# Decay order, seven half-depth products for the shared expert of chunks three and four, and reordered fills at the branch and in the second layer's first chunk

## The chip, the cores and the metric

One Trainium2 chip, of which the kernel uses one core. The metric is the device time of one execution in microseconds (us), the median of three runs. All values are fp32.

## The reference, cut to what matters

There are two layers over 2048 tokens (8 sequences of 256) of 512 features. Each layer normalizes its input and adds two branches to it, an attention and a mixture of experts.

```python
xn = _layernorm(x)
x = x + L0_attn(xn) + L0_ffn(xn)
xn = _layernorm(x)
x = x + L1_attn(xn) + L1_ffn(xn)
```

Layer 0's attention is linear attention with 32 heads of 128 in blocks of 32 tokens, with an exponential decay for each head (`exp(-slope * distance)`). Layer 0's FFN routes each token to two of 16 experts and adds a shared expert:

```python
logits = xt @ router_w + router_b
scores = softmax(logits) + router_bias     # then the best 2 of 4 groups, the best 2 experts in them
h = silu(xt @ w1 + b1) * (xt @ w2 + b2)    # for each expert, times its gate
...
z = silu(xt @ sw1 + sb1) * (xt @ sw2 + sb2) @ sw3 + sb3
```

The shared expert has `sw1` and `sw2` of 512 x 256: together one product of depth 512 and 512 columns for each token. Layer 1 has a softmax attention with one head of 128, and 64 low-rank experts of rank 16, of which each token takes 16:

```python
h = einsum('nd,krd->nkr', xf, A)
out = einsum('nkr,kdr->nd', h * G[:, :, None], B)
```

## The kernel before, in words

Tokens are worked in four chunks of 512 (`CH`), each of four tiles of 128 rows. TensorE (PE) multiplies 128x128 weights with up to 512 columns into PSUM banks, named ps_a (two), ps_b, ps_e, ps_sc (three) and ps_o. VectorE (DVE), ScalarE (ACT) and GpSimd (POOL) do the rest, and nearly all DMAs are issued by SyncE (SP), whose queue is served in the order written.

**The opening** (L144 to L495) is ordered by the tile scheduler: it weighs the instructions by its own costs, and only those under `keep_in_program_order` are held to the order of the code. For each chunk `normalize` (L264) centres and scales the rows, `turn` (L464) transposes them on TensorE (L279) and copies them to `xT` (DVE L284, ACT L282). `shared_up` (L365) computes the shared expert's two products with `project` (L358 to L363): four blocks of 128 features, each four matmuls 128x512 over the depth, 16 matmuls for a chunk; ACT takes silu with the bias (L375), DVE multiplies (L376). Between the blocks stand the router's `scores` (L312). `route` (L321) picks the two experts by a chain of some forty small DVE operations with one exponential on ACT. `share` (L393) and `shared_down` (L379, matmuls L384) make the shared expert's output one chunk later, add it to the rows and store it to `xr`. `decays` (L401) makes the heads' decays, `exp` of `dist` by ACT (L406), and stores them to DRAM in `dec`; `dist` itself is made by POOL (L219 to L235). `token_sums` (L413) makes sums of quarters of xT for the attention's products by sevens: POOL subtracts (L101 is the helper of every such operation), and the results go to DRAM in `xc` through `xsum` tiles, three of them (L449 and L455). For chunk one the results stay in SBUF as `xt`.

**Products by sevens.** A product of 2x2 blocks is done as seven products of blocks of half the size (p1 to p7) in place of eight, at the price of sums of the operands before and of the results after. The attention uses it in two levels (L745), the second layer in `seven` (L1418): each pass of it fills bank a with p1, ACT copies it, p2 fills bank b, p6 goes on top of p1 in bank a, ACT copies again, p7 fills bank e, and so on; `out_` adds bank and copy. Between the products `filled(k)` emits what a dictionary `fill` holds for place k: the work of other parts that is to run there.

**After the opening** a block (L670 to L1415) runs the heads and the experts with the order of ACT and POOL written by hand; the first heads' copies (L1122) of ps_a to `cp` start it. The experts' tiles are gathered by slot. There are up to 47 tiles, of which 36 (`USUAL`) are computed always, and the rest under a runtime branch, `beyond` (L1227, branch L1229), which is not taken with this input: its body of eleven experts is jumped over.

**Second layer** (from L1418). For each chunk `low_rank` (L1617) makes two passes of `seven` over A (matmuls L1629): `fill1` and `fill2` (L1682 to L1705) put into them the softmax gates (`head.gates`, L1582 and L1544), the transposes of the probabilities (`turned`, L1648), the product with the values (`weighed`, L1664) and the next chunk's sums; `spread_both` sends small DMAs that spread the gates (L1600). A last pass of `seven` over B follows (matmuls L1726). Chunk four's first-layer result is completed by `finish` (L650, the operation at L656) inside the first chunk's last pass (L1755 to L1763).

## Time and profile before

| | |
|---|---|
| three runs | 2737.56, 2741.88, 2747.89 us; median 2741.88 |
| profiled execution | 2735.27 us, its span 2733.6 us |
| granted TensorE clock, mean | 0.997 |
| TensorE | 2695.3 us busy, 99% of the span |
| DVE, ACT, POOL | 1590.8 (58%), 944.9 (35%), 1652.1 (60%) |
| DMA | 721.46 MB, mean 264 GB/s |
| attention's products by sevens, L745 | 5376 matmuls from ps_a's first group: 749.4 us |
| experts' second products, L957 | 1288 matmuls: 304.8 us |

In a row of the timeline stand the start in us, the time that the row covers, engine and line, the operation with output and input, the matmul's shape, and how many instructions of the kind follow each other (x8); square brackets give the idle time of the engine before it and who ended it. In a windows row stand the window, its length, then the busy time and the instructions in brackets for PE, PE's weight loads, DVE, ACT and POOL, then the granted clock, the DMA share and GB/s. A line by itself with an engine name and "q" is the engine's sequencer, with durations in ns (lowest, median, highest).

### The profile page before, as it was taken

To read this page: it belongs to the slowest core of one execution; us is meant where nothing else is said; L and a number is where in the kernel's file an instruction comes from. 1 tells how busy PE (TensorE), PEld (TensorE's weight loads), DVE (VectorE), ACT (ScalarE), POOL (GpSimd) and SP (SyncE) were. 2 spreads that over 40 slices of the span, in tenths; PEclk is the share of its full clock that TensorE was granted. 3 is DMA by queue.
4 is the path that set the end of the run, shared out by engine and by line. 5 is a ranking of instruction groups with operands and counts; after the bars stand their busy time and mean duration, and the time that the engine had idled before them with its cause. 6 is when DMAs were issued, how large, how long until landed. Compare 5 with 4: busy or idle time off the path is not lost. (4 is left out here: it accounts for less than half of the span.)

```text
span 2733.6 us, 48695 instructions
## 1 busy us (share of the span) xinstructions
PE 2695.3 (99%) x19250; PEld 2492.6 (91%) x19250; DVE 1590.8 (58%) x2701; ACT 944.9 (35%) x1672; POOL 1652.1 (60%) x1509
## 2 busy tenths in 40 slices
PE   9999999999999999999999999999999999999999
PEld 5699999999999999999999999999999999987877
DVE  7657777776545555555545555555554555667663
ACT  5232222222343333333443333334433333432221
POOL 6478777777466666666755555656655567653210
PEclk9999999999999999999999999999999999999999
DMA  7889888888988778768777777777776688663211
GB/s 293 313 331 343 298 344 330 327 322 332 338 303 290 270 272 284 255 248 297 293 251 262 252 260 253 268 287 259 281 267 234 245 303 308 219 220 106 72 64 64
DMA packets 150871, 721.46 MB, mean 264 GB/s; under 512 B 18240, under 2 KB 24768, under 8 KB 108096
## 3 DMA queue, kind: packets, MB, share of 16 engines
q1 hardware_dynamic: 135824, 661.89, 66.0%
q0 software_dynamic: 14528, 55.88, 6.1%
q8 instruction: 154, 2.52, 0.4%
q14 instruction: 77, 0.63, 0.1%
q10 hardware_dynamic: 288, 0.52, 0.1%
HBM read 576.29 MB, written 144.04 MB: 264 GB/s over the span
## 5 line engine op out<-in xcount | busy, mean ns | idle before, releaser
L745 PE MATMUL ps_a<-xt,w 128*128 128x128 f32 x5376 | 749.4, 276 | 6.9 <-POOL w L101 3.2
L745 PEld LDWEIGHTS ps_a<-xt,w 128*128 128x128 f32 x5376 | 685.7, 192 | 32.0 <-issue 14.6
L101 POOL TENSOR_TENSOR c<-c,r 128x512 f32<-128x512 f32 x264 | 362.1, 1397 | 158.5 <-DVE r L101 151.4
L1122 ACT COPY cp<-ps_a 128x512 f32<-128x512 f32 x384 | 224.6, 585 | 673.6 <-PE ps_a L745 633.5
L101 POOL TENSOR_TENSOR c<-c 128x512 f32<-128x512 f32 x240 | 305.9, 1287 | 248.6 <-DVE c L101 221.5
L745 PE MATMUL ps_e<-xt,w 128*128 128x128 f32 x2688 | 374.5, 275 | 0.2 <-DVE r L101 0.2
L101 POOL TENSOR_TENSOR sums<-sums,sq 128x256 f32<-128x256 f32 x240 | 181.0, 754 | 295.6 <-ACT sq L891 285.8
L745 PE MATMUL ps_a<-w,xt 128*128 128x128 f32 x1792 | 346.6, 275 | 0.0
L745 PEld LDWEIGHTS ps_e<-xt,w 128*128 128x128 f32 x2688 | 341.5, 192 | 4.5 <-issue 1.0
L101 POOL TENSOR_TENSOR w<-w 128x512 f32<-128x512 f32 x224 | 298.4, 1340 | 74.3 <-DVE w L101 28.1
L957 PE MATMUL ps_sc<-wo,gT 128*128 128x256 f32 x1288 | 304.8, 380 | 3.8 <-PEq L1229 3.4
L745 PEld LDWEIGHTS ps_a<-w,xt 128*128 128x128 f32 x1792 | 272.3, 192 | 0.0
L101 DVE TENSOR_TENSOR acc<-ps_sc,acc 128x512 f32<-128x512 f32 x208 | 142.6, 689 | 211.2 <-PE ps_sc L957 167.5
L957 PEld LDWEIGHTS ps_sc<-wo,gT 128*128 128x128 f32 x1288 | 232.4, 190 | 29.0 <-issue 3.5
L900 DVE SCALAR_TENSOR_TENSOR gT<-ps_o,nw,c 128x256 f32<-128x256 f32 x256 | 111.9, 478 | 219.6 <-ACT sq L891 219.0
L745 PE MATMUL ps_b<-xt,w 128*128 128x128 f32 x1536 | 214.9, 276 | 5.6 <-issue 3.5
L101 DVE TENSOR_TENSOR c<-ps_a,c 128x512 f32<-128x512 f32 x216 | 146.6, 686 | 114.6 <-PE ps_a L745 108.5
L891 ACT ACTIVATE sq<-ps_o 128x512 f32<-128x512 f32 x128 | 76.4, 597 | 380.5 <-PE ps_o L880 370.4
L745 PEld LDWEIGHTS ps_b<-xt,w 128*128 128x128 f32 x1536 | 195.6, 193 | 8.6 <-issue 5.2
L842 ACT ACTIVATE c<-c 128x512 f32<-128x512 f32 x256 | 150.1, 627 | 140.1 <-DVE c L101 106.3
L101 DVE TENSOR_TENSOR s<-ps_sc,decay 128x384 f32<-128x384 f32 x256 | 139.4, 552 | 79.6 <-PE ps_sc L868 78.2
L745 PE MATMUL ps_e<-w,xt 128*128 128x128 f32 x896 | 173.5, 275 | 0.0
(296 smaller groups left out, 4569.3 us busy)
## 6 DMA issues: line engine op xcount, KB each, us to landing
w<-in_w_att_dram SPq DMA_DIRECT2D x56, 1024.0 KB
w<-in_w_att_dram SPq DMA_DIRECT2D x72, 768.0 KB
st<-in_w_att_dram SPq DMA_DIRECT2D x32, 1024.0 KB
wo<-in_w_out_dram SPq DMA_DIRECT2D x113, 256.0 KB
decay<-dec SPq DMA_DIRECT2D x64, 384.0 KB
w<-ws0p SPq DMA_DIRECT2D x12, 1792.0 KB
w<-ws1p SPq DMA_DIRECT2D x12, 1792.0 KB
w<-ws2p SPq DMA_DIRECT2D x12, 1792.0 KB
```

Of the source, the lines that this page charges most:

```text
L101: (eng or nc.vector).tensor_tensor(o, a, b, op)
L745: mm(bank[:, bass.ts(ty, P)], a, b, start=(first and ty == 0), stop=True, skip_group_check=True,)
L842: nc.scalar.activation(qk, qk, AF.Silu)
L891: nc.scalar.activation(sq, po, AF.Square)
L900: nc.vector.scalar_tensor_tensor(gT[:, h, :].rearrange("p (t n) -> p t n", t=2), po[:, bass.ts(h, S)].rearrange("p (t n) -> p t n", t=2), ...
L957: mm(py[:, bass.ts(t, S)], self.O[p][:, hh, bass.ts(t, P)], self.wo[p][:, hh, :], start=(t == 0 and hh == 0), stop=(hh == 1), skip_group_c ...
L1122: nc.scalar.copy(c, bank)
```

## The change

- The router's bias tiles and a zero tile move from tiles of their own to parts of `disp` and `scratch`.
- Four sums of quarters of the shared expert's weights (`s1` to `s4`) are made by POOL at the start. `shared_up_sevens` does the shared expert's first product by sevens for chunks three and four (`i > 1`): seven products of four matmuls 128x256 in place of 16 matmuls 128x512. Chunks one and two keep `shared_up`. Its operand sums come from `token_sums`, which now makes the four sums of quarters first, into tiles of their own (`xo`, four of them), and sends them out in the order in which they are read; `xsum` has two tiles in place of three.
- Of the decays' activations the first is put under `keep_in_program_order`.
- The branch gets `preferred_fallthrough_block=False`: the comparison goes on to the case "not taken" and jumps to the body.
- In `seven` the fill of place 2 comes before `out_(0, 0)`. In the second layer's first chunk the gates move from place 1 to place 2, both probability transposes to place 7, `weighed` to places 3 and 4, and `spread_both` to place 2.
- `finish` of chunk four is kept in the order of the code.

```diff
@@ -163,9 +163,9 @@
     nc.sync.dma_start(out=rw, in_=router_w)
     bsh_t = once([P, 2, SH], "bsh_t")
     nc.sync.dma_start(out=bsh_t, in_=b_sh)
-    rb = once([P, 1, E], "rb")
+    rb = disp.tile([P, 1, E], FP, name="rb")
     nc.sync.dma_start(out=rb, in_=router_b.to_broadcast([P, E]))
-    rbias = once([P, 1, E], "rbias")
+    rbias = disp.tile([P, 1, E], FP, name="rbias")
     nc.sync.dma_start(out=rbias, in_=router_bias.to_broadcast([P, E]))
     for i in range(1, NCH):
         for t in range(TPC):
@@ -192,7 +192,7 @@
     xs_ = [dram.tile([P, TPC, C], FP, name=f"xs{i}") for i in range(NCH)]
     xr = [dram.tile([P, TPC, C], FP, name=f"xr{i}") for i in range(NCH)]
     table = dram.tile([NSLOT, SAME], I32, name="table")
-    none = once([P, NMT * SAME], "none", I32)
+    none = scratch[:, 2, 0 : NMT * SAME].bitcast(I32)
     nc.vector.memset(none, 0)
     nc.sync.dma_start(out=table.rearrange("(p j) o -> p (j o)", p=P), in_=none)
 
@@ -362,6 +362,83 @@
                 start=(c == 0), stop=(c == NC - 1),
             )
 
+
+    def w_part(n, j):
+        return wsh[:, bass.ts(j, NC // 2), bass.ts(n, SH * P)]
+
+    n = NC // 2 * SH * P
+    places_ = [held[:, SH * C + n * m : SH * C + n * (m + 1)] for m in range(2)]
+    places_ += [scratch[:, m, 512 : 512 + n] for m in range(2)]
+    s1, s2, s3, s4 = (v.rearrange("p (c n) -> p c n", c=NC // 2) for v in places_)
+    for o, a, b, f in (
+        (s1, w_part(1, 0), w_part(1, 1), ALU.add), (s2, s1, w_part(0, 0), ALU.subtract),
+        (s3, w_part(0, 0), w_part(1, 0), ALU.subtract), (s4, w_part(0, 1), s2, ALU.subtract),
+    ):
+        tt(o, a, b, f, nc.gpsimd)
+    WS = dict(p1=w_part(0, 0), p2=w_part(0, 1), p3=s4, p4=w_part(1, 1), p5=s1, p6=s2, p7=s3)
+    xsums = {}
+
+    def shared_up_sevens(i, between):
+        hT = scratch[:, 2 + i % 2, :].rearrange("p (e n) -> p e n", e=SH)
+        up, whole = {}, {}
+
+        def tile_():
+            return work.tile([P, CH], FP, tag="h1", name="h1", bufs=4)
+
+        def go(bank, p, first=False):
+            w, xx = WS[p], xsums[i][p]
+            for n in range(SH):
+                for c in range(NC // 2):
+                    mm(
+                        bank[:, bass.ts(n, S)], w[:, c, bass.ts(n, P)], xx[:, c, :],
+                        start=(first and n == 0 and c == 0), stop=(c == NC // 2 - 1),
+                        skip_group_check=True,
+                    )
+
+        def copied(bank):
+            c = tile_()
+            nc.scalar.copy(c, bank)
+            return c
+
+        def silu(b, o, v):
+            for e in range(SH):
+                at = bass.ts(e, S)
+                nc.scalar.activation(o[:, at], v[:, at], AF.Silu, bias=bsh_t[:, 0, e : e + 1])
+            up[b] = o
+
+        def gated(b, c):
+            for e in range(SH):
+                at = bass.ts(e, S)
+                nc.vector.scalar_tensor_tensor(
+                    hT[:, e, bass.ts(b, S)], c[:, at], bsh_t[:, 1, e : e + 1], up[b][:, at], ALU.add, ALU.mult
+                )
+
+        a = ps_a()
+        go(a, "p1", True)
+        c1 = copied(a)
+        between()
+        b = ps_b()
+        go(b, "p2", True)
+        tt(c1, b, c1, ALU.add)
+        silu(0, c1, c1)
+        between()
+        go(a, "p6")
+        c2 = copied(a)
+        e = ps_e()
+        go(e, "p7", True)
+        between()
+        go(a, "p5")
+        c4 = copied(a)
+        tt(c4, e, c4, ALU.add)
+        go(a, "p3")
+        silu(1, tile_(), a)
+        gated(1, c4)
+        between()
+        go(e, "p4")
+        tt(c2, e, c2, ALU.add)
+        gated(0, c2)
+        return hT
+
     def shared_up(i, between):
         hT = scratch[:, 2 + i % 2, :].rearrange("p (e n) -> p e n", e=SH)
         for e in range(SH):
@@ -370,7 +447,7 @@
             between()
             project(p2, wsh, SH + e, i)
             between()
-            h1 = work.tile([P, CH], FP, tag="h1", name="h1")
+            h1 = work.tile([P, CH], FP, tag="h1", name="h1", bufs=4)
             b1, b2 = bsh_t[:, 0, e : e + 1], bsh_t[:, 1, e : e + 1]
             nc.scalar.activation(h1, p1, AF.Silu, bias=b1)
             nc.vector.scalar_tensor_tensor(hT[:, e, :], p2, b2, h1, ALU.add, ALU.mult)
@@ -403,7 +480,9 @@
         for n in range(6 * i, min(6 * i + 6, H // 2)):
             d = work.tile([P, 2, S + P], FP, tag="decay", name="decay")
             for hh in range(2):
-                nc.scalar.activation(d[:, hh, :], dist, AF.Exp, scale=-SLOPES[2 * n + hh])
+                ins = nc.scalar.activation(d[:, hh, :], dist, AF.Exp, scale=-SLOPES[2 * n + hh])
+                if n + hh == 0:
+                    tc.keep_in_program_order(ins)
             nc.sync.dma_start(out=dec[n], in_=d)
 
     HC = NC // 2
@@ -419,29 +498,30 @@
             return v.rearrange("p (c t) n -> p c t n", c=2)
 
         def tile_():
-            return work.tile([P, 4, P], FP, tag="xsum", name="xsum", bufs=3)
+            return work.tile([P, 4, P], FP, tag="xsum", name="xsum", bufs=2)
 
         quarter = {
             (j, l): xT[i][:, bass.ts(j, HC), bass.ts(l, S)].rearrange("p c (t n) -> p c t n", t=2)
             for j, l in QUARTERS
         }
-        with_ = None
         if i == 0:
             for p in ORDER:
                 first_x[p] = toks.tile([P, 7, P], FP, tag="X", name="xt")
-        for p, at in (
-            ("p1", (0, 0)), ("p2", (1, 0)), ("p3", (1, 1)),
-            ("p5", (0, 1)), ("p6", (1, 1)), ("p4", (1, 0)), ("p7", (1, 1)),
-        ):
-            y = quarter[at]
-            if p in ("p5", "p6", "p4", "p7"):
-                o = {"p5": quarter[0, 0], "p7": quarter[0, 1]}.get(p, with_)
-                with_ = blocks(tile_() if i else first_x[p][:, 0:4])
-                sub(with_, y, o, nc.gpsimd)
-                y = with_
+        ys = {p: quarter[at] for p, at in (("p1", (0, 0)), ("p2", (1, 0)), ("p3", (1, 1)))}
+        sums = {}
+        for p, at, o in (("p5", (0, 1), (0, 0)), ("p6", (1, 1), "p5"), ("p4", (1, 0), "p6"), ("p7", (1, 1), (0, 1))):
+            sums[p] = first_x[p][:, 0:4] if i == 0 else work.tile([P, 4, P], FP, tag="xo", name="xo", bufs=4)
+            ys[p] = blocks(sums[p])
+            sub(ys[p], quarter[at], ys[o] if o in ys else quarter[o], nc.gpsimd)
+        if i:
+            xsums[i] = {p: xT[i][:, bass.ts(j, HC), bass.ts(l, S)] for p, (j, l) in dict(p1=(0, 0), p2=(1, 0), p3=(1, 1)).items()}
+            for p, t in sums.items():
+                xsums[i][p] = t.rearrange("p (c t) n -> p c (t n)", c=HC)
+        for p in ORDER:
+            y = ys[p]
             if i == 0:
                 t = first_x[p]
-                if y is not with_:
+                if p not in sums:
                     nc.sync.dma_start(out=blocks(t[:, 0:4]), in_=y)
                 if p in RAW:
                     first_sums.append(t)
@@ -481,7 +561,7 @@
                 nc.sync.dma_start(out=w[:, 0:4], in_=w_att[0, RAW[p]])
                 first_w.append(w)
         pl, tiles = ps_sc(), list(range(TPC))
-        ups.append(shared_up(i, lambda: scores(pl, xT[i], tiles.pop(0), lambda ins: tc.keep_in_program_order(ins) if i == 0 else ins)))
+        ups.append((shared_up_sevens if i > 1 else shared_up)(i, lambda: scores(pl, xT[i], tiles.pop(0), lambda ins: tc.keep_in_program_order(ins) if i == 0 else ins)))
         ge = disp.tile([P, TPC, E], FP, name=f"ge{i}")
         route(pl, ge, sel_all[:, bass.ts(i, TPC), :])
         gates.append(ge)
@@ -1226,7 +1306,7 @@
 
         def beyond():
 
-            with tc.If(n_used[0] > USUAL):
+            with tc.If(n_used[0] > USUAL, preferred_fallthrough_block=False):
                 for j in range(USUAL, NMT):
                     e = Expert(j)
                     e.turn()
@@ -1437,8 +1517,8 @@
         filled(1)
         b = ps_b()
         go(b, "p2", True)
+        filled(2)
         out_(0, 0, b, c1)
-        filled(2)
         go(a, "p6")
         c2 = copied(a)
         e = ps_e()
@@ -1621,7 +1701,8 @@
             def spread_both():
                 gates2.extend(spread(h * HJ + j) for h in range(2))
 
-            fill = {1: [*fill.get(1, ()), spread_both], **{k: f for k, f in fill.items() if k != 1}}
+            k = 2 if i == 0 and j == 0 else 1
+            fill = {**fill, k: [*fill.get(k, ()), spread_both]}
 
             def product(bank, w, xx, first):
                 for n in range(2):
@@ -1680,9 +1761,12 @@
             for n in range(TOP):
                 gather(i + 1, n, following[1 + n])
         fill1 = {
-            1: [head.gates] if i == 0 else [],
-            2: [partial(turned, 0)], 7: [partial(turned, 1)], 5: [partial(weighed, 0)], 3: [partial(weighed, 1)], 4: [],
+            1: [],
+            2: [head.gates if i == 0 else partial(turned, 0)],
+            7: [partial(turned, b) for b in range(i > 0, 2)], 5: [], 3: [], 4: [],
         }
+        for b, k in enumerate((5, 3) if i else (3, 4)):
+            fill1[k].append(partial(weighed, b))
         fill2 = {k: [partial(attended, t)] for t, k in enumerate((2, 7, 5, 3))}
         fill2[4] = []
         if following:
@@ -1757,7 +1841,7 @@
             x3 = spare8()
             nc.sync.dma_start(out=x3, in_=xr[NCH - 1])
             last_bias(x3, work.tile([P, C], FP, tag="sb3", name="sb3", bufs=1))
-            fill[4].append(partial(finish, NCH - 1, x3))
+            fill[4].append(partial(finish, NCH - 1, x3, range(TPC), tc.keep_in_program_order))
         seven(work, product, AB, XB, out_, fill)
         if i == 0:
             nc.sync.dma_start(out=xs_[NCH - 1], in_=x3)
```

## The prediction

> **What bounds the kernel now.** I read the page's busy times first, then TensorE's waits by line, then the windows stage by stage, and last the timeline around each place that the change touches.

> ```profile
> PE 2695.3 (99%) x19250; PEld 2492.6 (91%) x19250; DVE 1590.8 (58%) x2701; ACT 944.9 (35%) x1672; POOL 1652.1 (60%) x1509
> ```
> TensorE is busy for 2695.3 of 2733.6 us, so all its idle time together is 38.3 us. A reordering can win only from these; beyond them only matmul work, or time at a lower clock, can go. The windows put the idle time at some 6 us in the first 20 us, none from 20 to 120, 5.3 from 120 to 200, 3.8 around the branch and 4.2 around the second layer's first chunk:

> ```profile
> 0.00:20.00 20.00, 14.33 (x61) 10.39 (x62) 15.43 (x44) 10.41 (x18) 6.15 (x22) 0.91 0.88 308
> 20.00:120.00 100.00, 100.00 (x359) 54.89 (x358) 66.91 (x192) 39.97 (x61) 70.13 (x118) 0.98 0.79 298
> 2440.00:2520.00 80.00, 75.83 (x327) 58.22 (x326) 61.63 (x167) 18.41 (x37) 33.91 (x29) 0.98 0.49 169
> ```
> The change touches just these stretches. From about 200 to 2440 us the order of the instructions is the same in both, but for the branch.

> **The head.** The first shared product waits for xT's copies, which ACT does after four decay activations:

> ```profile
> 13.71 5.25 PE L360 MATMUL ps_b<-xT,wsh 128*128 128x512 f32 x8 [2.59 <-ACT xT L282]
> 10.94 1.76 ACT L406 ACTIVATE decay<-dist 128x384 f32<-128x384 f32 x4
> 12.61 1.05 ACT L282 COPY xT<-ps_a 128x512 f32<-128x512 f32 x2
> ```
> With one activation (0.44) in place of four (1.76) the copies come 1.3 us earlier. Against it, POOL gets four weight sums, each like its 128x512 op of 1.27 us (5.1 us), ahead of the last two operations that make `dist`; they wait for the shared weights. From the sums' landing (my estimate 7.5 to 8 us, by the load's place in the queue and 308 GB/s) `dist` is ready near 11.2 instead of before 10.9. That leaves −0.8 (from −1.3 to +0.3). The eight matmuls there run at half clock (5.25 against 3.60 us elsewhere); I let that stand.

> **The sevens, chunks three and four.** One 128x512 matmul costs 0.858 us between neighbours: 16 to a chunk are 13.73. The seven products are 28 matmuls 128x256; by half the columns 0.429 each, 12.01 in all. That is −1.72 a chunk, −3.4 in both. It assumes that no bubble comes between, and TensorE is at 100% here. So every wait that the new form adds counts in full, and it adds some. Before, each bank was read once by ACT and DVE; now bank a is drained three times by ACT in mid-product, and DVE must add a bank before it is free.

> ```profile
> 60.84 0.94 ACT L406 ACTIVATE decay<-dist 128x384 f32<-128x384 f32 x2 [2.64 <-DMA dec<-decay]
> 64.98 0.94 ACT L406 ACTIVATE decay<-dist 128x384 f32<-128x384 f32 x2 [3.21 <-DMA dec<-decay]
> 71.66 1.27 POOL L101 TENSOR_TENSOR xsum<-xT 128x512 f32<-128x512 f32 x1 [4.46 <-DMA xc<-xsum]
> ```
> (a) In the changed ACT order chunk three's first drain stands behind eight decay activations. Each pair waits for its buffer's store, and those stores share SP's queue with the token sums' stores, of which POOL now has two buffers instead of three. Before, the rows show such waits of 2.6 to 4.5 us that nobody on TensorE felt. Between nothing and 4, I take 1.0: the work in hand is mostly earlier than the bank's need. (b) DVE's add of p4 stands behind the whole routing chain of that chunk, and the next transposes want that bank. The chain ran before from 57.24 to 67.23 us on DVE, four shared adds of 0.68 among it, so 7.3 by itself, with a gap 7.5. TensorE has four transposes, one early product, p3, p4 and half a shared-down pair to do meanwhile: 0.6 + 0.4 + 1.7 + 1.7 + 0.9 = 5.3. I take the difference, 2.2 (0 to 4, as some of the chain may be done early, or start late with ACT's exponential). (c) The shared-down product of chunk three waits for four gating operations and an xT copy: 0.4. (d) In chunk four p7 waits for POOL's last sums, 0.4, and the shared-down product for the add behind the routing chain, whose part after p5 I count at 6.9 against the same cover: 1.6. Sum of the waits 5.6, ends −1 (a bank that frees earlier than before) and +10.

> [...] After the 1.84 us wait at 125.51 the next six matmuls took 1.49 instead of 0.83 us, and after the 2.20 us wait below the clock was half for 3.4 us:

> ```profile
> 125.51 1.15 PE L745 MATMUL ps_a<-xt,w 128*128 128x128 f32 x6 [1.84 <-ACT cp L1122]
> 126.88 1.49 PE L745 MATMUL ps_e<-xt,w 128*128 128x128 f32 x6
> 2461.00:2464.40 3.40, 3.40 (x13) 2.75 (x12) 0.75 (x2) 0.20 (x1) 1.94 (x2) 0.53 0.23 63
> ```
> [...] by the rows a wait of 1.8 to 2.2 can cost another 3.4 × 0.5 = 1.7. Such waits elsewhere passed without it, so I put the dip into the range (0 to two, +3.4), not the sum.

> **First units.** The first cp copy waits for a freed buffer, not for TensorE: it takes memory whose last reader is a store of chunk four's shared result. Now the 1 MB load of the first attention weights stands before that store in SP's queue: at 300 GB/s up to +3.3; but weights, first sums and outer sums come earlier, up to −2 with the 1.84 and part of its dip. I take 0, and keep −2 to +3.

> **The branch.**

> ```profile
> 2090.51 1.97 PE L957 MATMUL ps_sc<-wo,gT 128*128 128x256 f32 x8 [3.39 <-PEq L1229]
> L1229 PEldq COMPARE_BRANCH  x1: 4627/4627/4627, 2085.6 to 2085.6; - x1
> L1229 ACTq COMPARE_BRANCH  x1: 45/45/45, 2085.6 to 2085.6; - x1
> ```
> The comparison jumps over a body of eleven experts, and TensorE's takes 4.6 us where ACT's takes 0.045. In the changed program it falls through, into a block whose unconditional branch jumps over the same body. The row, read alone, would promise −3.4: no taken comparison, no 4.6 us. [...] The far jump stays, so I take 0; the other end is −3.4.

> **Second layer, first chunk.**

> ```profile
> 2456.43 1.46 PE L1629 MATMUL ps_a<-ts,fas 128*128 128x256 f32 x6
> 2460.08 0.30 PE L1648 MATMUL ps_sc<-ident,pb 128*128 128x128 f32 x1 [2.20 <-DVE pb L1576]
> 2461.14 2.77 PE L1629 MATMUL ps_e<-wsm,fa 128*128 128x256 f32 x6
> 2470.17 1.99 PE L1629 MATMUL ps_e<-t,fa 128*128 128x256 f32 x8 [0.30 <-DVE cp L101]
> ```
> All of p7 (8 matmuls, 1.8 us) now runs before the turned probabilities are wanted; the second tile's `pb`, ready near 2461.1, still leaves about 1.0 of the 2.2 us: −1.2. With the long wait split, the half clock after it goes: −1.7. Four L656 operations (4.7 us of DVE with their neighbours) leave this chunk, so the 0.30 goes as well. Sum −3.2 (−1 to −4.5). The long DVE row before it (3.78 us while POOL adds) is untouched. In chunk two those operations, and the 2 MB of xs traffic now ahead of the spread gates' small DMAs on SP, come back: DVE's spread waits, 4.2 us the longest, can grow by some 3 us, mostly under matmuls: +0.5 (0 to +3).

> **Sum.** −0.8 −3.4 +5.6 +0 +0 −3.2 +0.5 = −1.3 us. The profiled execution took 2735.27 us, 6.6 below the median, so it becomes about 2734.0, and the median 2741.88 − 1.3 = 2740.6.

> **The rivals.** (1) Likeliest, 0.58: small gains repaid by waits at the routing chain, 2740.6, own range 2735 to 2747. (2) The waits are hidden, because the scheduler's order fits the machine[...]: −0.8 −3.4 +1 −3.4 −3.2 = −9.8, or 2732; with the first unit's wait and its dip gone (−3.5) and the head's dip too, 2727. For it: ACT is at 40% and DVE at 67% in this stretch. Against: it needs the routing chain to yield to TensorE, and its place in DVE's order is fixed. 0.27. (3) Slower: the routing chain on DVE ahead of the p4 add. At (b) and (d) TensorE stands for the 4 us and 2.5 us at the upper ends, each with a half clock of 1.7, and the drain at (a) for 4: −0.8 −3.4 +4 +2.5 +3.4 +4 −2 +3 (the weights load before the store) = +10.7, so 2753. It decides from about 3 us per wait, as the sevens then lose more than head and second layer bring. 0.15. Against it: TensorE's cover of 5.3 us is real. Of (2) some part is that the branch edit does nothing: then it is 2735.

> **Chances.** A measurement tells 0.5% (13.7 us: under 2728.2, over 2755.6) from no change. Of (2) a third, with all ends good, gives 0.09 faster; of (3) half or so, with its ends over +13.7, gives 0.07 slower; the rest, 0.84, is within. The range reaches from 2729 in (2) to 2754 in (3).

> **What would show it.** In the trace after: TensorE's first L360 row near 12.9 instead of 13.71; seven-product rows of 0.43 a matmul, with waits on DVE `h1` (1.5 to 4 us) at the transposes and on ACT `h1` at p6; the branch row still above 4 us on PEldq; the wait at L1648's counterpart near 1.0 and the clock after it 1.0. I am wrong if the 20 to 120 stretch shows no idle TensorE, or if the branch's wait is gone: then it is 3 to 9 us less. I am wrong upward if waits at the new banks pass 3 us or cluster with half clocks.

## The result and the profile after

The changed kernel took 2754.43 us (median of 9 runs, 2750.65 to 2757.63) beside 2741.09 for the kernel before (9 runs, 2736.21 to 2747.89): ratio 1.0047, interval 1.0038 to 1.0056. I had forecast 2740.6 with a range up to 2754.0. So the change costs about 13 us where I had it gain one.

The profiled execution of the changed kernel took 2756.7 us (span 2754.6), against 2735.27 (span 2733.6) before. This pair lies further apart (21.4) than the medians. The page's first part and the windows after (columns: busy time and instructions of PE, PEld, DVE, ACT, POOL, then the granted clock, the DMA share, GB/s):

```profile
PE 2700.3 (98%) x19298; PEld 2505.0 (91%) x19298; DVE 1600.7 (58%) x2711; ACT 951.2 (35%) x1684; POOL 1655.0 (60%) x1513
```
```profile
20.00:60.00 40.00, 39.09 (x153) 22.29 (x152) 32.77 (x76) 21.22 (x32) 35.29 (x53) 0.96 0.67 255
60.00:90.00 30.00, 27.06 (x133) 20.03 (x131) 20.94 (x77) 17.88 (x30) 16.32 (x33) 1.00 0.87 328
90.00:120.00 30.00, 28.41 (x111) 18.96 (x111) 17.38 (x56) 10.01 (x16) 17.07 (x32) 1.00 0.66 252
120.00:140.00 20.00, 14.05 (x88) 11.95 (x87) 16.00 (x46) 2.66 (x5) 0.00 (x0) 0.91 0.89 306
```
TensorE's busy time grew by 5.0 us, its idle time from 38.3 to 54.3. The stretch from 20 to 120 us, which had no idle TensorE, now has 0.91 + 2.94 + 1.59 = 5.4 us, and 120 to 140 has 5.95. The first product starts at 13.78 instead of 13.71, so the head is as it was. TensorE's waits by line show whom it waited for (total, times, longest):

```profile
PE ps_sc L279 <- DVE spare L259: 7.2, 5, 2.2
PE ps_a L825 <- ACT cp L1202: 6.7, 3, 5.8
...
PE ps_e L279 <- DVE h L101: 1.7, 1, 1.7
PE ps_e L461 <- DVE h L101: 1.6, 1, 1.6
```
The two waits on DVE's `h` are those I had forecast at the seven products. The first two lines are the ones that I had not: cp at the first units (1.84 before, now 5.83) and the transposes of the second layer's results (0.59 and 0.57 before in chunks one and two, now 2.16 and 2.17).

**Where the 21 us lie in the two traces.** I matched TensorE's instructions of both traces, and set the stretches at half clock apart: such a stretch lasts 3.41 or 6.83 us at a granted clock of 0.50, and I count half of that as its cost where TensorE has work (in the one behind the branch eight matmuls took 3.75 us, before at full clock 1.97). Up to its last matmul there are 17.1 us at half clock before and 30.7 after, which makes 6.8 us. The stretch at the branch (from 2098.99) begins 1.35 us before TensorE goes on, so 6.1 of these are felt.

| Stretch | longer by | of it half clock |
|---|---|---|
| head, to the first product | 0.1 | 0 |
| shared stage, to the first unit | 3.8 | 0 |
| first units, to 230 us | 3.5 | 0 |
| 230 to 2090, many waits of 0.2 to 0.5 | 1.9 | 0 |
| branch | 3.2 | 2.7 |
| from there to the second layer | 1.0 | 0 |
| second layer | 7.6 | 3.4 |

**The same over all runs.** Each run has its span and its mean granted clock. Span times clock is roughly what the run would take at full clock; the rest of the span is lost to the clock. It is an estimate: TensorE isn't always the bound, half clock that falls on a wait is counted as lost though it costs nothing, and the clock is given to 0.001. But its mean over many runs separates two things that the medians mix. Before (51 runs): 2729.5 ± 0.4 at full clock (± is the standard error of the mean), 10.6 lost. After (9 runs): 2737.4 ± 0.7, and 15.0 lost. So of 12.2 us between the mean spans, 7.9 are work and waits, and 4.3 are lower clock. The table below uses this split. One run of the kernel without sevens, flag and layer 2 (3102.56 us) was in a slow state and is left out of it.

### The profile page after: what moved, and what is told of

Read it like the earlier page. It is cut to its first block, busy times and chain, and to the rows that moved or that the text cites. A ratio compares the mean times of both kernels' runs of the same rounds, so it can differ in the third digit from the quotient of the medians.

```text
span 2754.6 us, 48810 instructions
## 1 busy us (share of the span) xinstructions
PE 2700.3 (98%) x19298; PEld 2505.0 (91%) x19298; DVE 1600.7 (58%) x2711; ACT 951.2 (35%) x1684; POOL 1655.0 (60%) x1513
## 5 line engine op out<-in xcount | busy, mean ns | idle before, releaser
L825 PE MATMUL ps_a<-xt,w 128*128 128x128 f32 x5376 | 750.0, 276 | 10.7 <-ACT cp L1202 6.7
L101 POOL TENSOR_TENSOR c<-c 128x512 f32<-128x512 f32 x240 | 304.9, 1283 | 264.5 <-DVE c L101 216.6
L101 POOL TENSOR_TENSOR c<-c,r 128x512 f32<-128x512 f32 x264 | 361.0, 1392 | 162.5 <-DVE r L101 154.1
L101 POOL TENSOR_TENSOR sums<-sums,sq 128x256 f32<-128x256 f32 x240 | 181.4, 756 | 296.5 <-ACT sq L971 286.8
L101 POOL TENSOR_TENSOR w<-w 128x512 f32<-128x512 f32 x224 | 298.1, 1339 | 72.6 <-DVE w L101 27.9
L101 DVE TENSOR_TENSOR acc<-ps_sc,acc 128x512 f32<-128x512 f32 x208 | 142.6, 689 | 212.9 <-PE ps_sc L1037 169.6
L101 DVE TENSOR_TENSOR c<-ps_a,c 128x512 f32<-128x512 f32 x216 | 146.7, 686 | 112.0 <-PE ps_a L825 108.6
L101 DVE TENSOR_TENSOR s<-ps_sc,decay 128x384 f32<-128x384 f32 x256 | 139.5, 552 | 79.9 <-PE ps_sc L948 76.6
```

What stands on the lines that cost most here:

```text
L101: (eng or nc.vector).tensor_tensor(o, a, b, op)
L825: mm(bank[:, bass.ts(ty, P)], a, b, start=(first and ty == 0), stop=True, skip_group_check=True,)
```

## The experiments

All kernels were timed in five rounds beside the kernel before (its median was 2741.3 to 2742.1 each time, its mean at full clock 2729.1 to 2729.5). "Flag" is the branch's `preferred_fallthrough_block=False`, "layer 2" the new order of the second layer with `finish` kept in place. "Full" is the mean at full clock, "lost" what the clock took, both as above.

| Kernel | runs | median | ratio, interval | full | lost |
|---|---|---|---|---|---|
| before | 51 | 2742.05 | 1 | 2729.5 ± 0.4 | 10.6 |
| after | 9 | 2754.43 | 1.0047 (1.0038–1.0056) | 2737.4 ± 0.7 | 15.0 |
| after, no sevens | 15 | 2746.49 | 1.0017 (1.0010–1.0025) | 2731.9 ± 0.5 | 13.0 |
| after, layer 2 as before | 6 | 2748.54 | 1.0033 (1.0020–1.0045) | 2734.6 ± 0.5 | 12.8 |
| after, branch as before | 5 | 2750.60 | 1.0037 (1.0023–1.0051) | 2735.8 ± 1.3 | 14.9 |
| after, finish not kept in place | 5 | 2755.39 | 1.0051 (1.0037–1.0064) | 2737.6 ± 0.4 | 15.4 |
| after, last xr store on ACT | 5 | 2762.05 | 1.0073 (1.0059–1.0087) | 2741.0 ± 1.4 | 18.2 |
| after, two xr stores on ACT | 6 | 2749.44 | 1.0030 (1.0018–1.0042) | 2731.3 ± 0.8 | 17.4 |
| after, last xr store in four | 6 | 2755.87 | 1.0042 (1.0030–1.0055) | 2738.5 ± 0.6 | 13.8 |
| after, routing later | 11 | 2750.06 | 1.0024 (1.0016–1.0033) | 2732.9 ± 0.8 | 14.5 |
| after, xs store later | 5 | 2749.61 | 1.0039 (1.0025–1.0053) | 2735.2 ± 0.5 | 14.3 |
| after, four repairs | 6 | 2750.63 | 1.0033 (1.0021–1.0044) | 2735.2 ± 0.7 | 13.8 |
| before + flag | 13 | 2742.51 | 1.0001 (0.9993–1.0010) | 2729.2 ± 0.6 | 11.0 |
| before + decay order | 14 | 2741.30 | 0.9996 (0.9988–1.0005) | 2727.4 ± 0.5 | 11.9 |
| before + layer 2 | 14 | 2744.63 | 1.0012 (1.0002–1.0022) | 2731.2 ± 0.5 | 12.2 |
| before + decay order, layer 2, late xs store | 14 | 2741.50 | 0.9999 (0.9991–1.0007) | 2729.5 ± 0.4 | 10.6 |
| after, no sevens, flag and layer 2 | 21 | 2746.24 | 1.0015 (1.0007–1.0023) | 2730.9 ± 0.5 | 11.9 |
| the one above, last xr store in four | 13 | 2747.47 | 1.0021 (1.0013–1.0029) | 2733.5 ± 0.4 | 11.8 |

### Which part costs: the parts taken out, and put in alone

**Sevens out.** Chunks three and four use the old product again, and the weight sums go.

```diff
-    s1, s2, s3, s4 = (v.rearrange(...) for v in places_)   # and the four sums on GpSimd
-        ups.append((shared_up_sevens if i > 1 else shared_up)(i, ...
+        ups.append(shared_up(i, ...
```

> The changed kernel with the shared expert's first product of chunks three and four done as before (16 matmuls 128x512), and without the four sums of its weights. Theory A (the loss is spread over several places): the sevens' stage cost 3.9 us, and the 1 MB weights load that came to stand ahead of the last xr store another 4.0; both go, so the first attention matmul starts near 119.9 us instead of 123.8, TensorE's wait for the first cp copy falls from 5.8 to near 1.8 us, and the median from 2754.4 to about 2746.5; the head's first product starts near 12.5 us. Theory B (waits at the routing chain in the sevens are nearly the whole loss): back to the kernel before, 2741 within 2 us.

Measured 2746.49: the expected time, but in part by luck. The head gains: the first product starts at 12.28 instead of 13.78, so it was the weight sums that had held it. TensorE has one wait between 20 and 120 us (0.92). But the cp wait, which I expected at 1.8 again, is 5.05. So most of it doesn't come from the sevens.

**Layer 2 out.**

```diff
-        filled(2)
         out_(0, 0, b, c1)
+        filled(2)
...
-            k = 2 if i == 0 and j == 0 else 1
-            fill = {**fill, k: [*fill.get(k, ()), spread_both]}
+            fill = {1: [*fill.get(1, ()), spread_both], **{k: f for k, f in fill.items() if k != 1}}
```
(and `fill1` and `finish` as before)

> The changed kernel with the second layer's fills, the place of fill 2 in seven and the finish all as before. Theory A: TensorE's 2.2 us wait at the turned probabilities comes back (+3.4 with its half clock), but the waits of 2.2, 2.2 and 1.1 us at the next chunks' transposes and up to three half clocks go (-2.5 net of waits, -3.4 of clock): about 2749. Theory B: the second layer's change was a gain of 3 us by itself, so 2757.

Measured 2748.54, near the 2749 expected. The wait of 2.20 for the probabilities is back, and those at the transposes fall to 0.86, 0.57 and 0.50.

**Layer 2 alone, on the kernel before** (the reverse of that diff).

> The kernel before with only the second layer's reordering (fill 2 ahead of out_, gates, turns, weights and spread moved, finish kept in order). Theory A: the 2.2 us wait and its half clock go (-3.4), waits of 2.2, 2.2 and about 1 us at the next chunks' transposes with up to three half clocks come (+4.5 to +9): about 2745.5. Theory B: a gain by itself, 2738.5.

Measured 2744.63, and at full clock 1.6 ± 0.6 more than before. The transposes wait 2.16, 2.17 and 0.86. So the second layer's new order loses by itself, not only beside the sevens.

**Flag out, and flag alone.**

```diff
-            with tc.If(n_used[0] > USUAL, preferred_fallthrough_block=False):
+            with tc.If(n_used[0] > USUAL):
```

> The changed kernel with the branch as before (without the flag). In the five traces with the flag TensorE stands 3.9 to 4.3 us at the branch and then runs at half clock for 6.8 us; in the one trace without it 3.39 us and at full clock. Theory A (the second jump makes the idle time long enough for the clock to fall): idle 3.4 us, no half clock behind the branch, 0.5 + 3.4 us less: median about 2750.5. Theory C (the flag does nothing[...]): the wait stays within 0.3 us of 3.9 or the half clock comes all the same, median 2754 within 1.5.

> The kernel before with only the branch's flag set. Theory A: the idle time at the branch becomes 3.9 us or more, 6.8 us at half clock follow: 2741.6 + 3.9 = about 2745.5. Theory C: 2741.6 within 1.5, with a wait of 3.4.

Out of the changed kernel: 2750.60, the time of theory A. But A's sign is missing: after a wait of 3.27 the half clock came all the same, and at full clock (2735.8 ± 1.3 against 2737.4 ± 0.7) the two can't be told apart. Alone: 2742.51, which is no difference, so the theory that the flag costs some us falls. It does make the wait at the branch longer: the ten traces with the flag have 3.85 to 4.43, the eight without it 2.71 to 3.39. That is about 0.9 on average, too little for these times to show. Here is the row of the changed kernel's timeline, and what its sequencers' branch records say (count, then shortest, median and longest in ns):

```profile
2100.34 3.75 PE L1037 MATMUL ps_sc<-wo,gT 128*128 128x256 f32 x8 [3.92 <-issue]
L1309 PEldq COMPARE_BRANCH  x2: 95/1831/3567, 2094.9 to 2096.6; - x2
```
One long branch of 4.63 us became two, of 0.095 and 3.57: a long one is still there, now the second. The half clock after it (3.75 for eight matmuls, 1.97 before) also comes in six of the eight traces without the flag.

**Decay order alone**, on the kernel before: only the first activation keeps its place.

```diff
-                nc.scalar.activation(d[:, hh, :], dist, AF.Exp, scale=-SLOPES[2 * n + hh])
+                ins = nc.scalar.activation(d[:, hh, :], dist, AF.Exp, scale=-SLOPES[2 * n + hh])
+                if n + hh == 0:
+                    tc.keep_in_program_order(ins)
```

> The kernel before with only the first decay kept in order. First product at about 12.3 instead of 13.7 us; the first units unchanged (waits 1.8 and 1.1 us): 2741.9 - 1.4 = about 2740.5, by both theories; if the shift moves the order of the transfers at the first units, up to 3 more.

The first product starts at 11.93 instead of 13.71. The median, 2741.3, can't be told from before; at full clock it is 2.1 ± 0.6 less, and the clock takes 1.3 of that back.

**All but sevens, flag and layer 2**: what stays is the decay order, the moved tiles and the new order of the token sums.

> The changed kernel without sevens and weight sums, with the second layer and the branch as before: what is left is the kept first decay, the moved tiles and the token sums' new order with two xsum tiles. Theory F (the token sums' stores stand ahead of the first weights transfers in SP's queue): TensorE's two waits at the first attention products sum to about 6 us against 2.9 before, +3, with a half clock more +1.7, less 1.4 at the head: about 2745. Theory G (the token sums are neutral): 2740.5.

Measured 2746.24, as theory F had it, which gives this remainder a cost of its own. TensorE waits 4.69 for cp. Beside the decay order alone this kernel is 3.5 ± 0.7 more at full clock: that is the price of the token sums and moved tiles (no run separates these two), of which I had put none down.

### The first units: order of the queue, or bytes in flight?

The cp copy waits for a store of chunk four's shared result (`xr`) that frees its memory. The copy's row in the changed kernel names another transfer, the load `st`:

```profile
132.76 0.59 ACT L1202 COPY cp<-ps_a 128x512 f32<-128x512 f32 x1 [23.71 <-DMA st<-in_w_att_dram]
```
By the trace's landing records `st` is complete only at 134.9, after the copy. The store is complete at 132.47, 0.30 before it, and in all 18 traces the copy starts 0.1 to 0.5 us after that store. SP's issues in the changed kernel's timeline, and in that of before:

```profile
116.81 0.32 SPq L470 DMA_DIRECT2D xr<-x  x1
117.18 0.42 SPq L788 DMA_DIRECT2D ws0p<-w  x1
122.95 0.33 SPq L773 DMA_DIRECT2D w<-in_w_att_dram  x1
123.67 0.88 SPq L470 DMA_DIRECT2D xr<-x  x1
124.61 0.42 SPq L768 DMA_DIRECT2D st<-in_w_att_dram  x1
```
```profile
104.94 0.42 SPq L708 DMA_DIRECT2D ws0p<-w  x1
...
109.34 0.40 SPq L688 DMA_DIRECT2D st<-in_w_att_dram  x1
...
115.33 4.76 SPq L393 DMA_DIRECT2D xr<-x  x2
120.18 0.38 SPq L693 DMA_DIRECT2D w<-in_w_att_dram  x1
```
Before, `ws0p` and `st` left at 105 and 109, so that the last `xr` store (119.77) had only the load of `w` behind it: cp ran at 124.87, 5.1 us later. Now `ws0p` stands behind the token sums and an `xr` store until 117, and the last store (123.67) leaves with 1 MB of `w` before it and 1 MB of `st` right after it: cp runs at 132.76, 9.1 us later. The same window of both kernels, changed first, shows that the DMA engines have nothing to do some us earlier (share and GB/s at the end of the line), where before they were busy:

```profile
112.00:116.00 4.00, 3.65 (x9) 1.74 (x10) 3.33 (x9) 0.00 (x0) 0.00 (x0) 1.00 0.00 0
112.00:116.00 4.00, 4.00 (x11) 1.85 (x10) 3.79 (x21) 0.00 (x0) 2.73 (x5) 1.00 0.86 321
```

**The last store on another queue.**

```diff
-        tc.keep_in_program_order(nc.sync.dma_start(out=xr[i], in_=xs[i]))
+        tc.keep_in_program_order((nc.scalar if i == NCH - 1 else nc.sync).dma_start(out=xr[i], in_=xs[i]))
```

> The changed kernel with only the last xr store (chunk four's shared result) issued from ACT's queue instead of SP's, so that the attention's weights loads no longer stand ahead of it in its queue. Theory A: the store lands 4 to 5 us after its issue instead of 8.8, TensorE's wait for the first cp copy falls from 5.8 to 1 to 3 us, median about 2751. Theory B: the wait is paid elsewhere, median stays at 2754 within 1.5.

Measured 2762.05, a miss for both theories. The store left ACT's queue at 126.3 and landed at 136.9; TensorE waited 7.55. On ACT's queue it was not faster.

**Both late stores on ACT** (`i > 1` in that line), so that SP's loads pass.

> The changed kernel with the xr stores of chunks three and four issued by ACT, which is idle there. Moving the last one alone did not help: the loads and stores of 1 MB each were all issued between 117 and 126 us, because the xr store of chunk three, waiting in SP's queue for its data, held up the transfers behind it while the DMA engines stood still from 111 to 116 us. Theory A1 (the queue is held up): with both off SP the weights transfers start near 110 us, the DMA engines are busy in 112 to 116, TensorE's wait for the first cp copy falls from 5.8 to under 3 us, and one of the two half-clock windows after it goes: 2754.4 - 3 - 1.7 = about 2750. Theory A2 (only the bytes count, whichever queue and time): the wait stays above 5 us, median 2754 or more.

Measured 2749.44, the time of theory A1, but by luck. SP's loads now do go early, and the DMA engines are busy from 112 to 116 us (share 1.03). The cp wait is still 7.43: the last store left at 125.4, right behind `w` (124.7) and `st` (125.1), and landed at 135.8. So the theory of the held-up queue falls, and the one of the bytes in flight stands. At full clock this is nevertheless the lowest (2731.3) of the variants that keep every part of the change; no run shows why, and in the trace some of it is half clock that fell on the long wait. The clock takes 17.4 from it.

**The last store in four parts**, so that its memory comes free piece by piece.

```diff
-        tc.keep_in_program_order(nc.sync.dma_start(out=xr[i], in_=xs[i]))
+        for t in range(TPC) if i == NCH - 1 else (slice(0, TPC),):
+            tc.keep_in_program_order(nc.sync.dma_start(out=xr[i][:, t, :], in_=xs[i][:, t, :]))
```

> The changed kernel with the xr store of chunk four as four stores of 256 KB, each as soon as its tile is added, in place of one of 1 MB after the last tile. Which queue issues it made no difference; what went with it did: 2 MB of weights loads were issued within 1.3 us of it, against 1 MB in the kernel before, and all three landed together about 9 to 10 us later. Theory A2 (bytes in flight): three quarters of the store have gone by then, the rest lands 3 to 4 us after the last tile, TensorE's wait for the first cp copy falls from 5.8 to 2 us or less, half a window of low clock goes as well: 2754.4 - 4 to - 5.5 = about 2750. Theory D (the copy waits for the loads, not for the store): the wait stays above 5 us, 2754.

Measured 2755.87. The wait that the theory speaks of went as it says, but nothing was gained. The timeline of TensorE in this kernel:

```profile
132.79 0.94 PE L826 MATMUL ps_a<-xt,w 128*128 128x128 f32 x6 [1.89 <-ACT cp L1203]
...
144.90 0.91 PE L826 MATMUL ps_a<-xt,w 128*128 128x128 f32 x6 [3.73 <-issue]
```
The cp wait is 1.89, and 12 us later comes a wait of 3.73, at weights whose loads SP issued only from 132.18. The other three variants that shorten the first wait show the same pair: 2.24 and 4.21 (routing later), 1.62 and 3.74 (four repairs), 3.02 and 4.07 (the last kernel of the table). In the 60 us from the first unit TensorE is idle for 6.4 us here, against 8.5 in the changed kernel (there 5.83, and later 0.98 and 1.56) and 4.2 before. So about half of what the store's wait gave came back as a wait for the next data. The 2 us that were left over this trace lost between 300 and 600 us, where its waits are more and longer than the changed kernel's; why, I have not settled.

### The seven products: routing before the bank's add

**Routing later**: in chunks three and four the add of p4 and the start of the routing keep their places in the program's order, add first.

```diff
-        tt(c2, e, c2, ALU.add)
+        tc.keep_in_program_order(nc.vector.tensor_tensor(c2, e, c2, ALU.add))
```
(and the routing's first addition likewise)

> The changed kernel with the routing chains of chunks three and four kept behind the last add of the sevens on DVE. Theory A (these chains stand ahead of the bank's release): TensorE's waits of 1.7 us at chunk four's transposes and 1.6 us at the shared-down product go, -3.3, median about 2751; a new wait at chunk four's p4, now behind chunk three's chain, may take up to 2 back, and the routing table comes later. Theory E (the drains by ACT are as late as the adds by DVE): the waits move to ACT's copies and the median stays at 2754 within 1.5.

Measured 2750.06, near the 2751 expected. Both waits on DVE's `h` are gone, and at full clock it is 4.6 ± 1.0 less than the changed kernel, of which those waits were 3.3. This confirms the mechanism that I gave at (b) and (d). The first units changed too (cp wait 2.24, then 4.21 for weights), so the rest of the 4.6 can't be assigned.

### The second layer: what is late next

**Finish not kept in its place**, so that the scheduler may put the four closing operations of the last chunk where it likes.

```diff
-            fill[4].append(partial(finish, NCH - 1, x3, range(TPC), tc.keep_in_program_order))
+            fill[4].append(partial(finish, NCH - 1, x3))
```

> The changed kernel with chunk four's finish not kept in the order of the code, so that its four operations, and with them the xs store and load of 1 MB each, go back into the second layer's first chunk. Theory A: the spread gates of chunk two land 5 us earlier, TensorE's wait of 2.17 us at chunk three's transposes falls to about 0.6 and the half clock after it goes: 2754.4 - 1.6 - 1.7 = about 2751, less if the first chunk pays for the four operations again (up to +2). Theory B: no change, 2754 within 1.5.

Measured 2755.39, theory B's time. The waits at the transposes fell to 0.58 and 0.57 as expected, but the timeline has a new one:

```profile
2484.29 2.07 PE L1745 MATMUL ps_o<-pT,v 128*128 128x256 f32 x4 [5.65 <-DVE pT L1733]
```
The four operations now stand before `pT` on DVE. DVE has this work to do in one place or the other, and each place costs TensorE a wait.

**The xs store later**: the store of the last chunk follows the second chunk's products, not the first chunk's.

```diff
-        if i == 0:
-            nc.sync.dma_start(out=xs_[NCH - 1], in_=x3)
...
         low_rank(2, fill2)
+        if i == 1:
+            tc.keep_in_program_order(nc.sync.dma_start(out=xs_[NCH - 1], in_=x3))
```

> The changed kernel with the 1 MB store of chunk four's first-layer result put behind chunk two's spread gates in the order of the code instead of ahead of them (it is read only a chunk later). Theory A: the gates land about 2.5 us earlier, TensorE's wait of 2.17 us at chunk three's transposes falls below 1 us and its half clock goes: 2754.4 - 1.3 - 1.7 = about 2751.5. Theory B (these waits are covered): 2754 within 1.5.

Measured 2749.61, 2.2 ± 0.9 less at full clock than the changed kernel; the intervals of the ratios overlap. The wait of 2.17 in chunk two fell to 0.61; chunk one's stayed (2.17).

**The same store moved, with decay order and layer 2, on the kernel before.**

> The kernel before with the kept first decay, the second layer's reordering, and the xs store of 1 MB behind chunk two's spread gates. Theory A: head -1.4; second layer -3.4 for the first chunk, one wait of 2.2 us with its half clock left of the three (+3.3): about 2740.5. Theory B: 2737.

Measured 2741.5, level with before. It has the decay order's gain and still 2.16 at both transposes. Here the moved store did not shorten the second one, so the store is not its only cause. From the issue of chunk two's gates to their first use it takes 8.1 us here, where it took 7.1 in the run above and 10.3 in the changed kernel. What else holds them I have not settled.

### Repairs together

**Four repairs on the changed kernel**: the store in four, the xs store later, no flag, and `dist` ahead of the weight sums on GpSimd:

```diff
-    nc.gpsimd.tensor_copy(dist[:, S : S + P], dist[:, 0:P])
+    tc.keep_in_program_order(nc.gpsimd.tensor_copy(dist[:, S : S + P], dist[:, 0:P]))
...
-        tt(o, a, b, f, nc.gpsimd)
+        tc.keep_in_program_order(nc.gpsimd.tensor_tensor(o, a, b, f))
```

> The changed kernel with three repairs at once and the branch as before: the weight sums kept behind the last operation that makes dist on POOL (head 1.3 us earlier, first product near 12.3 us), the xr store of chunk four in four pieces (-4 to -5.5), the xs store behind the spread gates (-1.3 to -3). Theory A: the places add up, 2754.4 - 8.5 = about 2746; the sevens themselves (waits 5.4 us for 1.5 us less matmul time) keep it above the kernel before by about 4. Theory B: 2750 or more.

Measured 2750.63, not the 2746 expected. The head gains (first product at 12.03), but the drain that I feared at (a) has come. The timeline of ACT in this kernel:

```profile
67.70 1.98 ACT L484 ACTIVATE decay<-dist 128x384 f32<-128x384 f32 x4 [5.05 <-DMA dec<-decay]
69.59 0.56 ACT L400 COPY h<-ps_a 128x512 f32<-128x512 f32 x1
```
The copy that drains the bank stands behind four decay activations, these wait 5.05 for their buffer's store, and TensorE waits 4.30 and then runs eight matmuls at half clock (3.75). In the changed kernel that store came sooner (2.47 for the same activations), and the drain cost nothing. The 1.75 us won at the head cost some six here.

**The last store in four, without sevens, flag and layer 2**: the diff of that store on the kernel that leaves these three out.

> The kernel before with what of the change paid: the first decay kept in order, the zero and bias tiles moved, the token sums' new order, without weight sums, sevens, flag and the second layer's reordering, and chunk four's xr store in four pieces. Theory A: head -1.4 us, the first cp copy's wait 1.8 us shorter or more, its half clock perhaps gone: about 2738. Theory B: same as before, 2741 within 1.5.

Measured 2747.47, a miss by 9. It waits 3.02 for cp (4.69 without the edit) and then 4.07 for weights, and is 2.5 ± 0.6 more at full clock than without it. No kernel that I ran is faster than before by its interval; decay order alone is level in time.

## Why the prediction was wrong

I forecast −1.3, as many small gains repaid by waits. The steps that failed are five: `dist` at 11.2 in the head, a wait's cost taken as its idle time alone in the sevens, the first units put at 0, the second layer put at −2.7, and half clock left out of the sum. Point by point, in the numbers of the two traces:

**The head (−0.8; came 0.1).** The step that failed is "`dist` is ready near 11.2". The decay row in ACT's timeline of the changed kernel, and GpSimd's timeline:

```profile
12.24 0.52 ACT L483 ACTIVATE decay<-dist 128x384 f32<-128x384 f32 x1 [1.44 <-POOL dist L235]
```
```profile
8.67 1.52 POOL L101 TENSOR_TENSOR held<-wsh 128x512 f32<-128x512 f32 x1 [6.17 <-DMA wsh<-in_w_sh_dram]
10.16 0.58 POOL L231 TENSOR_SCALAR_AFFINE_SELECT dist<-dist 128x256 f32<-128x256 f32 x1
10.71 1.26 POOL L101 TENSOR_TENSOR held<-held,wsh 128x512 f32<-128x512 f32 x1
11.93 0.28 POOL L235 COPY dist<-dist 128x128 f32<-128x128 f32 x1
```
The weights landed at 8.67 and not at 7.5 to 8, and the two operations that make `dist` stand behind one sum each: `dist` is ready at 12.2. The fewer activations are worth 1.8 us when nothing holds them (decay order alone: 11.93), and the sums took all of it.

**The sevens (−3.4 + 5.6 = +2.2; the stage came 3.8 longer).** The sum of the waits came out, 5.6 forecast and 5.4 in the windows, in part by luck. (b) and the 1.6 of (d) came as 1.69 and 1.59, and by the mechanism that I gave. The timelines of TensorE and DVE around the end of chunk three's product:

```profile
87.89 0.66 PE L279 MATMUL ps_e<-ident,xn 128*128 128x128 f32 x4 [1.69 <-DVE h L101]
```
```profile
86.85 0.38 DVE L101 TENSOR_TENSOR disp<-disp 128x16 f32<-128x16 f32 x2
87.15 0.68 DVE L101 TENSOR_TENSOR h<-ps_e,h 128x512 f32<-128x512 f32 x1
```
DVE does the last of the routing (`disp`), then the add of p4, and only then the bank is free for the transposes. But the drain at (a), 1.0 in my sum, and p7's 0.4 cost nothing, and the 0.4 of (c) came at chunk two's shared-down product, for a copy of xT alone. In place of the rest stand two waits that I did not have: 0.84 for DVE's add of chunk one's shared rows, which frees bank a, and 0.83 for DVE's gating in chunk two, which the kernel without sevens has as well (0.92).

The term "28 matmuls by 0.429", −3.4, nearly held. A matmul of the code stands as two in the rows, so a product of four is a row of x8. From start to next start such a product takes 1.72 to 1.83 us. All fourteen take 24.8 us, where the eight groups of the old product take 28.0 before: 3.2 saved. What failed is that I counted a wait by its idle time and the joints between products at nothing:

```profile
61.64 1.88 PE L461 MATMUL ps_a<-held,scratch 128*128 128x512 f32 x4
64.37 1.99 PE L392 MATMUL ps_a<-xT,wsh 128*128 128x256 f32 x8 [0.84 <-DVE x L101]
```
From 61.64 to 64.37 are 2.73 us. Such a group takes 1.72 to the next start when work follows at once (58.50 to 60.22 before), so the wait costs 1.01 where 0.84 is shown as idle: in these rows consecutive groups overlap by the other 0.17, and at a wait they don't. By this, and by more changes from one kind of product to another, the shared-down products, transposes and router scores of the stage take 1.7 us more than before, without their waits. So the stage is 5.4 − 3.2 + 1.7 = 3.9 longer, 3.8 from the first product on.

**First units (0; came +3.5).** I had the load of the first weights delay the store by up to 3.3 and set it off against an earlier start. The store did wait, but because all that SP holds back behind the token sums' stores and chunk three's `xr` store is then in flight together. The kernel without sevens, flag and layer 2 shows the wait with 4.69, so most of it belongs to the token sums' order with the moved tiles; I had looked at those stores as something that ACT waits for, and not as what stands before the loads on SP.

**The branch (0; came +0.5, and +2.7 of half clock).** Right for the wait (3.92 where it was 3.39): TensorE's sequencer still has a long branch (3.57 us, where my sign was "above 4"). That the wait would stay though the comparison falls through was an estimate of mine; the rows show how long the branch took, and not why.

**Layer 2 (−3.2 + 0.5 = −2.7; came +4.2, and +3.4 of half clock).** The step that failed is the +0.5 for the gates' transfers, put on chunk two alone and "mostly under matmuls". The first-chunk gain was there: between the products' start and the transposes TensorE came 4.7 us earlier than before, with the 2.20 wait at 0.66 and its half clock gone. It then met DVE, which waits for the spread gates. SP's issue of the gates and their first use on DVE, before and in the changed kernel, then TensorE's timeline in the changed kernel:

```profile
2463.03 2.63 SPq L1600 DMA_DIRECT2D spread_g<-gd  x4
2470.04 0.68 DVE L101 TENSOR_TENSOR hg<-cp,spread_g 128x512 f32<-128x512 f32 x1
```
```profile
2476.49 13.31 SPq L1680 DMA_DIRECT2D spread_g<-gd  x8
2482.03 0.69 DVE L101 TENSOR_TENSOR hg<-cp,spread_g 128x512 f32<-128x512 f32 x1 [3.78 <-DMA spread_g<-gd]
```
```profile
2503.92 1.11 PE L279 MATMUL ps_sc<-ident,spare 128*128 128x128 f32 x8 [2.16 <-DVE spare L259]
...
2579.20 1.12 PE L279 MATMUL ps_sc<-ident,spare 128*128 128x128 f32 x8 [2.17 <-DVE spare L259]
```
Before, the transposes waited 0.59 and 0.57. The gates' DMA was issued at the same moment of the stage as before (2463.03, against 2476.49 less the offset of 13.47), so it did not come earlier with TensorE. In chunk two SP has the xs store and load (2545.30, 2545.80) ahead of the gates (2546.22), and from that issue to DVE's first use it takes 10.3 us instead of 5.4. I had seen that mechanism and priced it at +0.5, since it would lie "mostly under matmuls"; it lay under them but for 1.6. In this trace half clock followed each of the two waits above 2 us (3.41 us of it from 2505.2 and from 2580.3), and also a third group of waits in chunk three (1.09, 0.92 and 0.84, then 3.41 us from 2658.8); in that of layer 2 alone it followed neither of the same two waits (2.16, 2.17). My sentence "the half clock after it goes" was true of one place and made me blind to three new ones. The run with the later xs store shows the link in chunk two: DVE's wait for the gates fell from 3.41 to 2.20, and TensorE's from 2.17 to 0.61. For chunk one it is read from these rows alone.

**Half clock (in the range, not in the sum; came +4.3 over all runs).** With layer 2's part it is the largest miss. I took it as an accident, though in the trace before there is half clock behind waits of 1.84 and 2.20, and the 2.2 that I had summed and those of layer 2 (2.16, 2.17) are of that size. The waits that came in place of my 2.2 and 1.6, of 1.69 and 1.59, were followed by none in the changed kernel's trace.

**The rivals.** The third, "slower", was nearest in time (2753), by the weights' load before the store and by half clocks. Its place was wrong: waits at the routing chain did not exceed what I had in the sum. A sum over the runs at full clock: decay order −2.1, token sums and moved tiles +3.5, layer 2 with the flag +1.0, sevens +5.5 (1.5 of these at the head), together 7.9. The steps depend on the order in which they are added: layer 2 is 2.8 when taken out of the whole, and the sevens 3.7 when put in without it. Each has an error of 0.7 to 0.9, so the split between those two stays open.

## What to carry to other kernels

With TensorE at 98 to 99%, ask of each stage that you shorten what feeds the next one, and when that is issued: here TensorE came 4.7 us earlier, the gates' transfer did not move along, and waits of 2.16 and 2.17 took its place. Of a reordered step, list the stores and loads too, each behind what it then stands in its queue, and what bytes are in flight beside the one that somebody waits for. And where the traces show half clock behind waits of some size (here 1.84, 2.16, 2.17 and 2.20), count a new wait of that size with the clock's price, as a chance times 1.7 us (half of 3.41), in the sum and not in the range.

## What was not expected of the hardware

An estimate from the two traces: a grid laid at all phases over their gaps, with 54% idle as the limit, has 2.9 windows above it before and 5.4 after on average. 2.5 times 1.7 is 4.2 us, where the runs lost 4.3. The limit is a choice of mine within the 45 to 60% of the counts (50% gives a difference of about 1.6 windows, 60% one of 2.2), and only the difference fits: 2.9 windows are 5 us, and the kernel before loses 10.6. This was counted afterwards, and no run was made to test it. The spread of one kernel's runs goes along with the clock: those of before at 2735.0 to 2738.5 have a mean clock of 0.997 or 0.998, and those above 2746 one of 0.994 to 0.996.

**The last `xr` store took longer with more in flight.** From the issue of the last 1 MB `xr` store to its landing it takes 4.8 to 5.4 us in the six traces where only the 1 MB load of `w` leaves behind it (4.8 before, 119.77 to 124.57), 7.7 and 8.0 where a load of 1 MB is in flight already and another follows, 8.6 to 8.9 with `w` before and `st` after it (8.8 in the changed kernel, 123.67 to 132.47), and 10.4 and 10.6 on ACT's queue behind both loads. Whether ACT's queue by itself adds to this, no run separates.
